# A software-pipelined graph-attention and expert kernel: other ranks for its phases, a lazier start, and a tail that begins one pair and one dense job per step

## The chip, the cores and the metric

The kernel runs on one NeuronCore of a Trainium2 chip. The metric is the time on the device in microseconds, from the first to the last instruction of the slowest (here the only) core; the time of a kernel is the median of several executions.

## The reference

Two layers are applied to x, 64 batches of 256 nodes with 256 features. `adj` is one 256 x 256 adjacency matrix for all batches. Cut to what matters:

```python
x = x + L0_gnn(layernorm(x), adj, W0, a0)     # 4 heads of 64, leaky slope 0.2, ELU at the end
x = x + layernorm(x) @ weight.T + bias        # 256 -> 256
x = x + L1_gnn(layernorm(x), adj, W1, a1)     # 1 head of 256, slope 0.01, ReLU at the end
x = x + L1_ffn(layernorm(x), router, w1, b1, w2, b2)

def gnn(h, adj, W, a):                        # per head
    q = h @ W
    e = leaky_relu(q @ a_src [:, None] + q @ a_dst [None, :])
    attn = softmax(where(adj, e, -huge), axis=-1)
    return act(attn @ q)

def L1_ffn(tokens, router, w1, b1, w2, b2):   # 8 experts, the best two of each token
    probs = softmax(tokens @ router.T); rw, re = top_k(probs, 2); rw = rw / rw.sum(-1)
    out = tokens
    for e in range(8):
        out = out + combine[:, e] * (gelu(tokens @ w1[e] + b1[e]) @ w2[e] + b2[e])
```

All is in float32.

## The kernel before

**Two kinds of work.** 62 of the 64 batches are *routed*: after the layers their rows are sent by indirect transfers to a buffer in device memory, `xs`, ordered by expert. Each token appears there twice. From that buffer *pairs* of tiles (256 rows of one expert) are read, run through the expert and added into the output rows by indirect transfers that add. There are 131 pairs. The last two batches are *dense*: every one of the 8 experts is applied to all of their rows, and the products are summed on chip, which makes 16 dense jobs.

**Steps, jobs and ranks.** Nothing is left to a scheduler. Each batch, pair or dense job is a Python generator; a loop of steps advances every active generator by one piece per step. What a generator yields is its *rank* in the next step: pieces of one step are emitted in the order of their ranks, smaller ones first, and jobs of equal rank in the order in which they began. The order of emission is the order on each engine's queue. A batch begins in every third step (`TICKS = 3`, in the step with phase 2), so in one step seven or so batches are worked on, each three pieces behind the one before it.

The pieces of a batch (`batch_layers`) and the step phase in which each falls, with the names that the profile shows:

| piece | phase | what it does | main instructions |
|---|---|---|---|
| 0 | 2 | transpose of the loaded blocks | DVE xT<-xblk L447 |
| 1 | 0 | statistics of x0 | DVE L314, L315; POOL rstd L322, L323 |
| 2 | 1 | projection of layer 0, then exp and scaling | PE pq L343; ACT q L351; DVE q L355 |
| 3, 4 | 2, 0 | scores of heads 0 and 1, of heads 2 and 3 | PE pd L410; DVE z L417 |
| 5 | 1 | attention times values, division | PE pv L431; DVE rinv L438, hp L464 |
| 6 | 2 | ELU and residual: x1, and x1 with the bias | ACT e L470; DVE x L473, L474, x1b L476 |
| 7 | 0 | statistics of x1, its transpose | PE pt L329; ACT xT L333 |
| 8 | 1 | the linear layer: x2, its statistics | PE pf L484; DVE x L490 |
| 9 | 2 | transpose of x2 | PE pt L329; ACT xT L333 |
| 10 | 0 | projection of layer 1 | PE pq L375; ACT ex L382, q L383, me L388 |
| 11, 12 | 1, 2 | scores and attention of layer 1 | PE pd L394, pv L431; DVE z L399 |
| 13, 14 | 0, 1 | ReLU; residual and statistics | ACT rel L506; DVE x L510 |
| 15, 16 | 2, 0 | scale and shift; normalized rows xng, and base | DVE by L515; ACT L524, L529 |
| 17, 18 | 1, 2 | base to the output, transpose of xng; logits | PE pt L329, pl L550; DVE lg L554 |

After piece 18 the last batch of a chunk routes the chunk (`route`): the two best experts of each token (`top_two`, some 12 small VectorE instructions), positions and pair numbers (some 50 more), then two sends per 128 rows on GpSimd (L816). Most chunks have four batches.

A pair (`expert_pair`) takes a load of its rows xr (L674), one step later a load of the expert's weights we (L685), then the transposes px (L692) and ScalarE's copy sT (L696), `hidden` (PE ph L724, ACT hT L730), `result` (PE py L739, DVE y L745), the scaling of y (ACT L717), and two adding scatters (POOL L756). Both scatters of a pair wait until the two scatters before them have landed, since rows may repeat from pair to pair. There are 7 buffers for y, 5 for xr and 7 for weights. A dense job (`dense_expert`) loads weights, runs `hidden` and `result`, and adds into `base` (DVE L782).

**The loop.** In a step of phase 2 it begins a batch, up to two waiting pairs (three once all batches have begun) and up to two dense jobs.

PSUM is one ring of 8 banks, taken in turn by pq, pd, pv, pt, pf, pl, ph, py and px.

**Before the loop** the masks, both layers' weights with their score columns (`gnn_weights`), the linear weights' transpose (`wfT`) and the router's transpose are prepared, all ahead of the first batch.

Of the kernel before, what the change touches and what calls it, by code (L numbers as in the profile page):

```python
# [20 lines left out]
def rows_to_all(ap: bass.AP, n: int) -> bass.AP:  # L21

    return bass.AP(tensor=ap.tensor, offset=ap.offset, ap=[[0, P], [1, n]])
# [3 lines left out]
def kernel(  # L27
# [84 lines left out]
    AHEAD, BLOCKS_AHEAD = 3, 2  # L112
    xblk = {0: load_blocks(0)}
    xin = {0: load_batch(0)}

# [12 lines left out]

    masks = []
    for layer, op in enumerate((ALU.is_gt, ALU.not_equal)):  # L130
        mf = work.tile([P, NT, N], F32, tag="xT", name=f"maskf{layer}", bufs=4)
        nc.vector.tensor_scalar(mf, adj_i, 0.0, None, op0=op)
        pm = bank("pm", [NT, N])
        for t in range(NT):
            for j in range(NT):
                nc.tensor.transpose(
                    pm[:, j, t * P : (t + 1) * P], mf[:, t, j * P : (j + 1) * P], ident
                )
        m = const.tile([P, NT, N], F32, tag=f"mask{layer}", name=f"mask{layer}")
        nc.vector.tensor_copy(m, pm)  # L140
        masks.append(m)

# [9 lines left out]
    def gnn_weights(w, a, heads, slope, name):  # L152

        d = D // heads
        wx = const.tile([P, KT, heads, d + 3], F32, tag=name, name=name)  # L160
        for k in range(KT):
            nc.sync.dma_start(
                out=wx[:, k, :, :d],
                in_=w[k * P : (k + 1) * P, :].rearrange("p (h d) -> p h d", h=heads),
            )
        av = work.tile([P, 2, d], F32, tag="e", name=name + "_a", bufs=1)
        nc.scalar.dma_start(out=av.rearrange("p s d -> p (s d)"), in_=rows_to_all(a, 2 * d))
        prod = work.tile([P, heads, d], F32, tag="hp", name=name + "_p", bufs=1)
        for k in range(KT):
            for s, c in ((0, d + 1), (1, d)):  # L170
                nc.vector.tensor_mul(
                    prod, wx[:, k, :, :d], av[:, s : s + 1, :].to_broadcast([P, heads, d])
                )
                nc.vector.tensor_reduce(wx[:, k, :, c : c + 1], prod, AX.X, ALU.add)
            nc.vector.tensor_scalar(
                wx[:, k, :, d + 1 : d + 2], wx[:, k, :, d + 1 : d + 2], 1.0 - slope, None,
                op0=ALU.mult,
            )
            nc.vector.tensor_scalar(
                wx[:, k, :, d + 2 : d + 3], wx[:, k, :, d : d + 1], slope - 1.0, None,  # L180
                op0=ALU.mult,
            )
        flat = wx.rearrange("p k h c -> p k (h c)")
        center(flat, heads * (d + 3))
        return flat

    wx0 = gnn_weights(w0, a0, H, SLOPE0, "wx0")
    wx1 = gnn_weights(w1g, a1g, 1, SLOPE1, "wx1")

# [4 lines left out]
    wfT = const.tile([P, KT, D], F32, tag="wfT", name="wfT")  # L194
    pw = bank("pw", [KT, D])
    for t in range(KT):
        for k in range(KT):
            nc.tensor.transpose(
                pw[:, k, t * P : (t + 1) * P], wf_in[:, t, k * P : (k + 1) * P], ident
            )  # L200
    nc.vector.tensor_copy(wfT, pw)
    center(wfT, D)

    bias_f = const.tile([P, D], F32, tag="bias_f", name="bias_f")
    nc.scalar.dma_start(out=bias_f, in_=rows_to_all(bf, D))
    nc.vector.tensor_scalar(bias_f, bias_f, -1.0, None, op0=ALU.add)

    r_in = work.tile([E, D], F32, tag="x1b", name="r_in", bufs=1)
    nc.scalar.dma_start(out=r_in, in_=router)
    rT = const.tile([P, KT, E], F32, tag="rT", name="rT")  # L210
    pr = bank("pr", [KT, E])
    for k in range(KT):
        nc.tensor.transpose(pr[:, k, :], r_in[:, k * P : (k + 1) * P], ident[:E, :E])
    nc.vector.tensor_copy(rT, pr)

# [41 lines left out]
    def fill_spare():  # L257
# [8 lines left out]
        yield 90  # L266


    setup = [lambda e=e: pack_expert(e) for e in range(E)] + [fill_spare]

# [65 lines left out]
    def projected(xT, wx, heads, rstd):  # L336
# [13 lines left out]
        for t, pq in enumerate(pqs):  # L350
            nc.scalar.activation(  # L351
                q[:, t, :, d:], pq[:, :, d:], AF.Exp, scale=rstd[:, t : t + 1]
            )
        for t, pq in enumerate(pqs):
            nc.vector.scalar_tensor_tensor(  # L355
                q[:, t, :, :d], pq[:, :, :d], rstd[:, t : t + 1],
                q[:, t, :, d : d + 1].to_broadcast([P, heads, d]), op0=ALU.mult, op1=ALU.mult,
            )
        return q

# [80 lines left out]
    def batch_layers(b, c0, xng, lg):  # L441
# [5 lines left out]
        nc.vector.transpose(xT.rearrange("p k n -> p (k n)"), xb.rearrange("p k n -> p (k n)"))  # L447
        yield 15
        x0 = xin.pop(b)
# [3 lines left out]
        yield 20  # L453
        q = projected(xT, wx0, H, rstd)
        yield 10
# [7 lines left out]
        for t, pv in enumerate(pvs):  # L463
# [3 lines left out]
            )  # L467
        yield 20
        ex = work.tile([P, NT, D], F32, tag="e", name="e", bufs=1)
# [26 lines left out]
        xT = transposed(x2)  # L496
        yield 40
        q, ex, me = projected1(xT, rstd, b)
        yield 10
        z = scores1(ex, me)  # L500
# [32 lines left out]
        xng.append(xe)  # L533
        yield 35
        if not dense:
# [9 lines left out]
        xT = transposed(xe[:, :, :D], *(("xTd", DENSE) if dense else ()))  # L545
        yield 50
        pl = bank("pl", [NT, E])
# [111 lines left out]
    def expert_pair(j, n, ids, ef, regs, needs):  # L659
# [27 lines left out]
        )  # L687
        yield 40
        px = bank("px", [KT, PAIR])
# [114 lines left out]
    active = []  # L804
    waiting, dense_jobs = [], []
    sent = []

    def begin(job, rank):
        active.append([rank, len(order), job])
        order.append(job)  # L810
# [16 lines left out]
    def later(rank):  # L827

        yield rank
        while (len(order_steps) - 1) % TICKS == 0:  # L830
            yield rank

    def route(c, row0, nt, n, last, xng, lg):

        rt = lambda shape, name, bufs=2, dt=F32: chunk_tile(shape, name, c, bufs, dt)
        vec, tt = nc.vector, nc.vector.tensor_tensor
        ohs, first, ed = top_two(c, nt, lg)
        m = rt([E, nt], "m")
# [131 lines left out]
    batches = jobs()  # L970
    step, more, credit = 0, True, 0.0
    SETUP_AT = 4
    with tc.manual_schedule():
        while more or active or waiting or dense_jobs or scatters:
            phase = step % TICKS
            if phase == 2 and more:
                nxt = next(batches, None)
                more = nxt is not None
                if more:
                    begin(nxt, 25)  # L980
            if step >= SETUP_AT and setup:
                begin(setup.pop(0)(), 90)
            if phase == 2:
                credit = min(credit + (2.0 if more else 3.0), 3.0)
# [12 lines left out]
            order_steps.append(step)  # L997
            for entry in sorted(active, key=lambda a: a[:2]):
                entry[0] = next(entry[2], None)
            if half_done:  # L1000
                finish_norms(NT)
            active[:] = [a for a in active if a[0] is not None]
            step += 1

# [34 lines left out]
```

The softmax here doesn't subtract the row's maximum and nothing guards it: scores larger than these inputs give would overflow.

## Time and profile before

| | |
|---|---|
| median of 3 executions | 1779.86 us (1778.52 to 1787.77) |
| span of the profiled execution | 1763.1 us, mean granted TensorE clock 0.945 |
| PE (TensorE) busy | 1559.9 us, 88% |
| PEld (weight loads, overlapping PE) | 1379.3 us, 78% |
| DVE (VectorE) busy | 1286.8 us, 73% |
| ACT (ScalarE) busy | 898.6 us, 51% |
| POOL (GpSimd) busy | 840.5 us, 48% |
| the first projection on TensorE (L343) starts | 27.25 us |
| the last send (L816) starts | 1537.86 us |

In the profile's lines PE is TensorE, PEld its weight loads, DVE VectorE, ACT ScalarE, POOL GpSimd and SP SyncE, which issues most loads. "L474" is a line of the kernel. A timeline row has its start, the busy time, engine, line, operation, output<-inputs and a count; in brackets stands the idle time just before it and who ended it. A row of waits reads: who waited for whom, microseconds in total, times, longest. Busy time of TensorE is no measure of peak speed, since matmuls overlap.

### The profile page before, as it was taken

The page shows a single profiled execution, that of the slowest core. Times are in us where ns is not written, and L with a number is a line of the kernel's source. Part 1 is how long each engine was busy: PE and PEld are TensorE (multiplying, and loading weights), DVE is VectorE, ACT ScalarE, POOL GpSimd, SP SyncE. Part 2 cuts the span into 40 slices and gives each one's busy share as a digit, 9 for nine tenths or more (in the row PEclk, how much of TensorE's full clock was granted, in tenths as well). Part 3 has the DMA queues.
Part 4 walks back from the last instruction along what each step waited for, and adds up shares of the span by engine and source line. Part 5 has one row for each costly group of instructions (what it writes and reads, how often), then busy time and mean ns, then how long its engine had stood idle before and what let it go on. Part 6 is the DMA issues. An engine that isn't in the chain of part 4 may idle for free. (4 is left out here: it accounts for less than half of the span.)

```text
span 1763.1 us, 29661 instructions
## 1 busy us (share of the span) xinstructions
PE 1559.9 (88%) x8998; PEld 1379.3 (78%) x8998; DVE 1286.8 (73%) x4744; ACT 898.6 (51%) x1965; POOL 840.5 (48%) x790
## 2 busy tenths in 40 slices
PE   5788788789999999999999999999989999678792
PEld 4677677678898979898888888888878888567682
DVE  4788888888878787879796878789888876522231
ACT  0234333445565656565656565656556566443241
POOL 0111233434646565646464555646565555734444
PEclk8899888999999999999999999999999899888896
DMA  5611122344656555555555564645564446585663
GB/s 139 183 37 47 50 67 77 76 119 97 137 124 139 130 138 125 119 136 112 130 123 139 123 148 112 150 113 126 128 147 119 101 111 152 126 219 116 146 132 44
DMA packets 272542, 209.67 MB, mean 119 GB/s; under 512 B 153849, under 2 KB 226561, under 8 KB 272385
## 3 DMA queue, kind: packets, MB, share of 16 engines
q1 hardware_dynamic: 221760, 139.40, 28.9%
q0 software_dynamic: 49632, 67.39, 20.7%
q8 instruction: 74, 1.21, 0.3%
q10 hardware_dynamic: 992, 0.99, 0.2%
q14 instruction: 84, 0.68, 0.1%
HBM read 118.55 MB, written 89.15 MB: 118 GB/s over the span
## 5 line engine op out<-in xcount | busy, mean ns | idle before, releaser
L756 POOL DMA_INDIRECT out_dram<-y,to x262 | 420.2, 1604 | 323.5 <-DMA out_dram<-y,to 124.8
L431 PE MATMUL pv<-q,z 128*128 128x65 f32 (+1 forms) x2560 | 371.4, 301 | 9.2 <-DVE y L745 9.1
L431 PEld LDWEIGHTS pv<-q,z 128*128 128x128 f32 x2560 | 341.3, 197 | 26.1 <-DVE y L745 11.1
L322 POOL TENSOR_SCALAR rstd<-mv 128x4 f32<-128x4 f32 (+1 forms) x132 | 46.3, 350 | 511.8 <-DVE mv L315 420.2
L724 PE MATMUL ph<-sT,we 128*128 128x256 f32 x1048 | 251.0, 396 | 41.3 <-ACT sT L696 22.8
L816 POOL DMA_INDIRECT xs<-xng,pos x248 | 251.0, 1012 | 69.1 <-issue 67.5
L739 PE MATMUL py<-w2s,hT 128*128 (+1 forms) x1176 | 264.3, 380 | 0.0
L724 PEld LDWEIGHTS ph<-sT,we 128*128 128x128 f32 x1048 | 204.8, 200 | 71.0 <-ACT sT L696 23.7
L739 PEld LDWEIGHTS py<-w2s,hT 128*128 128x128 f32 x1176 | 223.9, 191 | 30.7
L417 DVE SCALAR_TENSOR_TENSOR z<-pd,q,mask 128x256 f32<-128x256 f32 x512 | 209.8, 472 | 6.8 <-PE pd L410 6.8
L745 DVE TENSOR_TENSOR y<-py,b2s 128x512 f32<-128x512 f32 x147 | 98.2, 689 | 150.3 <-PE py L739 96.3
L730 ACT ACTIVATE hT<-ph,we 128x256 f32<-128x256 f32 x294 | 123.2, 470 | 165.6 <-PE ph L724 125.8
L333 ACT COPY xT<-pt 128x512 f32<-128x512 f32 x192 | 112.1, 584 | 162.7 <-PE pt L329 162.7
L717 ACT ACTIVATE y<-y,w 128x256 f32<-128x256 f32 x262 | 113.4, 500 | 119.4 <-DVE y L745 119.4
L314 DVE BATCH_NORM_STATS2 stats<-x 128x6 f32<-128x256 f32 x384 | 155.0, 404 | 2.2
L329 PE MATMUL pt<-ident,x 128*128 128x128 f32 x512 | 85.9, 292 | 75.7 <-DVE x L474 73.9
L375 PE MATMUL pq<-wx,xT 128*128 128x259 f32 x512 | 140.4, 422 | 0.9 <-ACT xT L333 0.9
L323 POOL TENSOR_TENSOR rstd<-rstd,mhalf 128x4 f32<-128x4 f32 (+1 forms) x132 | 135.4, 1025 | 11.0
L343 PE MATMUL pq<-wx,xT 128*128 128x268 f32 x512 | 130.0, 398 | 2.3 <-DVE wt L226 2.3
L484 PE MATMUL pf<-wfT,xT 128*128 128x256 f32 x512 | 131.7, 403 | 0.0
L329 PEld LDWEIGHTS pt<-ident,x 128*128 128x128 f32 x512 | 62.7, 156 | 85.8 <-issue 42.1
L470 ACT ACTIVATE e<-hp 128x512 f32<-128x512 f32 x64 | 40.3, 630 | 160.4 <-DVE hp L464 160.4
(155 smaller groups left out, 2488.5 us busy)
## 6 DMA issues: line engine op xcount, KB each, us to landing
we<-wpack SPq DMA_DIRECT2D x147, 288.0 KB, 5.2
xr<-xs SPq DMA_DIRECT2D x131, 260.0 KB, 3.7
xblk<-in_x_dram SPq DMA_DIRECT2D x256, 64.0 KB, 3.6
xin<-in_x_dram SPq DMA_DIRECT2D x64, 256.0 KB, 4.1
out_dram<-base SPq DMA_DIRECT2D x64, 256.0 KB, 3.6
out_dram<-y,to POOLq DMA_INDIRECT x262, 4.3
xs<-xng,pos POOLq DMA_INDIRECT x248, 2.6
xs<-fill SPq DMA_DIRECT2D x9, 260.0 KB, 4.3
```

The source lines that it names most:

```text
L314: nc.vector.bn_stats(stats[:, t, :], src[:, t, :])
L323: nc.gpsimd.tensor_tensor(rstd[:, :n], rstd[:, :n], mhalf[:, :n], ALU.pow)
L329: nc.tensor.transpose(pt[:, k, t * P : (t + 1) * P], src[:, t, k * P : (k + 1) * P], ident)
L343: nc.tensor.matmul(pq.rearrange("p h c -> p (h c)"), xT[:, k, t * P : (t + 1) * P], wx[:, k, :], start=(k == 0), stop=(k == KT - 1),)
L375: nc.tensor.matmul(pq, xT[:, k, t * P : (t + 1) * P], wx1[:, k, :], start=(k == 0), stop=(k == KT - 1),)
L417: nc.vector.scalar_tensor_tensor(z[:, j, :], pd[:, i, :], q[:, j, h, d + 2 : d + 3], mask[:, j, :], op0=ALU.max, op1=ALU.mult,)
L431: nc.tensor.matmul(pv[:, h, :], z[:, j, t * P : (t + 1) * P], q[:, j, h, : d + 1], start=(j == 0), stop=(j == NT - 1),)
L484: nc.tensor.matmul(pf[:, t, :], xT[:, k, t * P : (t + 1) * P], wfT[:, k, :], start=(k == 0), stop=(k == KT - 1),)
L724: nc.tensor.matmul(ph[:, f, :], we[:, k * D + f * P : k * D + (f + 1) * P], xT[:, k, :], start=(k == 0), stop=(k == KT - 1),)
L739: nc.tensor.matmul(py[:, t, :], hT[:, f, t * P : (t + 1) * P], w2s[:, e, f * D : (f + 1) * D].rearrange("p e c -> p (e c)"), start=(f == 0 ...
L756: d = nc.gpsimd.indirect_dma_start(out=out_rows, out_offset=bass.IndirectOffsetOnAxis(ap=to[:, t : t + 1], axis=0), in_=y[:, t, :], in_off ...
L816: d = nc.gpsimd.indirect_dma_start(out=xs_d[: E * CAP * PAIR, :], out_offset=bass.IndirectOffsetOnAxis(ap=at, axis=0), in_=xe, in_offset=None,
```

## The change

Three things are edited.

1. *Other ranks.* Several pieces get another rank, so that the order within a step changes. The pieces, their contents and their step phases stay. In phase 2 the ELU and residual (piece 6) now come first, ahead of the scores; the logits come ahead of layer 1's attention; `top_two` goes to the end of the step. In phase 0 layer 1's projection comes ahead of the transpose of x1, and the statistics of x1 ahead of those of x0. In phase 1 layer 0's projection comes ahead of layer 1's scores, the scaling of q behind them (a negative rank: the job is put back into the same step's queue), attention comes ahead of the transposes of xng and of the pairs' rows.
2. *A lazier start.* The layer-0 weights are loaded before the first blocks of x; the linear weights, layer 1's score columns, the second mask and the router are prepared as jobs of the first steps, beside the first batch, and the packing of the experts begins three jobs later.
3. *The tail.* Once every batch has left its layers, each step begins one waiting pair and one dense job, where before up to three pairs and two dense jobs began in every third step.

```diff
@@ batch_layers
         nc.vector.transpose(xT.rearrange("p k n -> p (k n)"), xb.rearrange("p k n -> p (k n)"))
-        yield 15
+        yield 40
...
-        q = projected(xT, wx0, H, rstd)
+        q, pqs = projected(xT, wx0, H, rstd)
+        yield -28
+        scaled(q, pqs, H, rstd)
         yield 10
...
-        yield 20
+        yield 5
         ex = work.tile([P, NT, D], F32, tag="e", name="e", bufs=1)
...
         xT = transposed(x2)
-        yield 40
+        yield 20
         q, ex, me = projected1(xT, rstd, b)
-        yield 10
+        yield 25
         z = scores1(ex, me)
...
         xng.append(xe)
-        yield 35
+        yield 55
...
         xT = transposed(xe[:, :, :D], *(("xTd", DENSE) if dense else ()))
-        yield 50
+        yield 35
@@ expert_pair
-        yield 40
+        yield 60
         px = bank("px", [KT, PAIR])
@@ route
+        yield -90
         ohs, first, ed = top_two(c, nt, lg)
@@ before the loop
-    setup = [lambda e=e: pack_expert(e) for e in range(E)] + [fill_spare]
+    setup = [
+        lambda work=work: once(work)
+        for work in (prepare_f, prepare1, lambda: fill_mask(1, ALU.not_equal), prepare_r)
+    ]
+    setup += [lambda e=e: pack_expert(e) for e in range(E)] + [fill_spare]
...
-    wx0 = gnn_weights(w0, a0, H, SLOPE0, "wx0")
-    wx1 = gnn_weights(w1g, a1g, 1, SLOPE1, "wx1")
+    wx0, prepare0 = gnn_weights(w0, a0, H, SLOPE0, "wx0")
+    xblk = {0: load_blocks(0)}
+    xin = {0: load_batch(0)}
+    prepare0()
+    wx1, prepare1 = gnn_weights(w1g, a1g, 1, SLOPE1, "wx1")
@@ the loop
-    step, more, credit = 0, True, 0.0
-    SETUP_AT = 4
+    step, more, credit = 2, True, 0.0
+    SETUP_AT = 3
...
-            if phase == 2:
+            if not more and not layers:
+
+                for jobs_left in (waiting, dense_jobs):
+                    if jobs_left:
+                        begin(jobs_left.pop(0)(), 90)
+            elif phase == 2:
                 credit = min(credit + (2.0 if more else 3.0), 3.0)
...
-            for entry in sorted(active, key=lambda a: a[:2]):
+            queue = [(a[0], a[1], a) for a in active]
+            heapq.heapify(queue)
+            while queue:
+                *_, entry = heapq.heappop(queue)
                 entry[0] = next(entry[2], None)
+                if entry[0] is not None and entry[0] < 0:
+                    entry[0] = -entry[0]
+                    heapq.heappush(queue, (entry[0], entry[1], entry))
```

## The prediction

> **What bounds the kernel now.** I read the page's slices first (where is an engine full), then the busy time by stretch, TensorE's own waits, the timeline of one batch before the experts begin, and the chain of waits at the end.
>
> The page's slices:
> ```profile
> PE   5788788789999999999999999999989999678792
> ...
> DVE  4788888888878787879796878789888876522231
> ```
> TensorE (PE) is the fullest engine from the tenth slice on. Before that it is at 7 or 8 tenths, with VectorE (DVE) as full as it.
>
> Busy time by stretch; I cut at the batches' hp multiplies (L464), at the last send and at the last matmul:
> ```profile
> 43.30:106.80 63.50, 51.29 (x295) 43.91 (x294) 48.63 (x145) 18.05 (x46) 8.20 (x14) 0.88 0.52 136
> 106.80:177.70 70.90, 59.76 (x388) 52.34 (x387) 59.37 (x191) 28.99 (x73) 10.06 (x16) 1.00 0.21 48
> 177.70:381.60 203.90, 166.26 (x976) 143.52 (x976) 170.31 (x622) 79.83 (x192) 65.63 (x78) 0.88 0.28 75
> 381.60:1440.00 1058.40, 1015.37 (x6103) 910.15 (x6102) 869.46 (x3206) 638.15 (x1367) 592.32 (x544) 0.98 0.53 126
> ...
> 1541.00:1727.00 186.00, 157.17 (x730) 136.48 (x730) 52.89 (x168) 71.38 (x159) 79.56 (x51) 0.90 0.65 148
> ```
> The columns are length, PE, PE weight load, DVE, ACT, POOL, clock, DMA. TensorE idles 12.2 + 11.1 + 37.6 = 61 us in the first three, 43 us in the long fourth (4%: TensorE is the bound there), and 29 us in the tail.
>
> TensorE's waits:
> ```profile
> PE pt L329 <- DVE x L474: 73.9, 37, 5.7
> ...
> PE px L692 <- DMA xr<-xs: 11.3, 15, 1.7
> PE pv L431 <- DVE y L745: 9.1, 11, 1.8
> PE pd L394 <- ACT ex L382: 9.0, 37, 0.4
> ```
> One wait stands out: the transpose of x1 waits for VectorE to finish x1. The timeline of one batch shows why:
> ```profile
> 128.39 1.62 DVE L417 SCALAR_TENSOR_TENSOR z<-pd,q,mask 128x256 f32<-128x256 f32 x4
> ...
> 130.95 0.69 DVE L474 SCALAR_TENSOR_TENSOR x<-e,x 128x512 f32<-128x512 f32 x1
> ...
> 131.79 0.63 PE L329 MATMUL pt<-ident,x 128*128 128x128 f32 x4 [2.15 <-DVE x L474]
> ...
> 141.25 0.18 DVE L438 RECIPROCAL rinv<-pv 128x4 f32<-128x4 f32 x1 [1.58 <-PE pv L431]
> ```
> VectorE does four score products (1.62 us) before x1, TensorE stands 2.15 us, and later VectorE stands 1.06 us for q's exponential (L355, further down the same timeline) and 1.58 us for TensorE's pv. Neither is full: the loop pv, hp, x1, transpose, pv (7.7 us on VectorE, 9.5 on TensorE) sets the 17.25 us of a batch.
>
> The end of the chain of waits:
> ```profile
> 1739.47 0.71 issue
> 1740.19 1.55 POOL out_dram L756
> 1741.74 0.30 issue
> 1742.04 3.85 DMA out_dram<-y,to
> ```
> Each pair's two adding scatters wait for those before them: 1.55 + 0.30 + 3.8 + 0.8 = 6.45 us a pair.
>
> **What the Trainium skill says.** "TensorE: Matmul & The Clock Gate", step-by-step of a matmul: only weight loads are pulled ahead, matmuls stay in program order. The trace agrees: pq (L375) stood behind the waiting transpose though its xT was copied at 129.82. So the order of emission matters. Same page, clock gate: after an idle window of about 3.4 us the clock halves. The trace agrees in sign: clock 1.00 where the gaps are 2.15 us, 0.88 at 177.7 to 381.6, where gaps of 5.71 and 3.52 us occur. "PSUM — Partial Sum Buffer", specifications: 8 banks, all of which the kernel rotates through, so a matmul also waits for the reader eight allocations back. "DMA: Bandwidth & Descriptors", anatomy of a SWDGE DMA: a fixed part of some 2 us, mostly the write receipt, which fits a scatter chain that more work elsewhere cannot shorten; here a landing takes 3.8 us.
>
> **The change, part by part.** The order of instructions in the two built programs shows what moves. No arithmetic of a batch, pair or dense job is added or removed.
>
> *x1 moves ahead of the score products (rank 20 to 5), and the second projection pq ahead of x1's transpose (40 to 20 against 30).* x1 is ready 1.62 + 0.3 us earlier, and needed 1.9 us later (pq is 8 matmuls, 1.92 us in the timeline). 3.8 us covers the usual gaps of 0.64 to 2.2 us and most of the 5.7. The whole row of 73.9 us should nearly go.
>
> *What takes its place.* pq now follows the transpose of x2 with only four pd transposes (0.44 us) between, and needs ScalarE's copy of it: about 0.67 us where the two stood next to each other (at 1470), so 0.23 to 0.35 us a batch; the low end is 15 us over 64 batches, the high end 22. I take 0.3: 19 us, 13 of it in the stretch 381.6 to 1440. The scores' product now waits in VectorE's order behind x1, but its reader pv comes two steps later: nothing.
>
> *pv ahead of the transposes of xng and px (35 to 55, 40 to 60).* pv's banks now follow those of the projection, not those of py, so its wait for y (9.1 us) goes. px runs some 4 us later relative to its load, so the 11.3 us on xr mostly go. pd (L394) runs after the other projection, and its 9.0 us go. q's scaling (the negative rank) still stands behind the scores product, with the same 1.06 us for ScalarE. In this step the projected and attended batches differ, so pv does not wait for it.
>
> *Stretch 43 to 382.* Batches without routing: VectorE's floor is 17.25 - 3.09 idle + 1.06 = 15.2 us, TensorE's 14.5 + 0.3; together about 15.7, 1.5 less a batch, 10 us for seven. With routing, four batches take 79.7 us now with VectorE busy 66.2; its floor with 1.06 each is 70.4, and I take 74: 5.6 per four, 14 us for ten batches. Sum 24; nothing extra for the clock.
>
> *Stretch 382 to 1440.* Four batches take 92.4 us, TensorE busy 88.5. Of 3.9 idle I expect 1.7 to stay (0.3 each, and VectorE full in the routing batch): 2.2 times 11 is 24 us; I take 22.
>
> *Start.* The first projection ran at 27.25. Now the layer-0 weights are loaded first, and the wf, wx1, mask1 and router preparations run as jobs beside batch 0. The projection can start near 15, but VectorE must still do wx1 (about 4.4 us in the old timeline) and mask1 before the second score products; pv starts near 32 instead of 36.3. 4 us.
>
> *Tail.* 31 pairs go through the scatter chain after 1539; 30 steps of 6.45 are 193.5 us, they took 214. So 20 us are gaps, mostly where a burst of three filled the y buffers and the queue of loads stood behind (TensorE 11.6 us at 1655, 8.0 at 1603). One pair and one dense job a step spreads this: SyncE's load waits no longer hold five weight loads. But a step then costs TensorE 3.94 + 3.50 = 7.44 us for one pair while the 14 remaining dense jobs last, 1 us more than the chain, hidden only by queued pairs. Ends: 20 gained, 0 or a few lost. I take 8.
>
> Sum: 24 + 22 + 4 + 8 = 58 us of 1780: 1722.
>
> **Rivals.** (a) *The wait moves.* TensorE's new wait for the copy costs 0.67 instead of 0.3 (24 us more), or VectorE, with 170 of 204 us busy, is the true bound early, and gains there halve (12): 58 - 36 leaves 22, about 1758. For it: VectorE idles only 1.83 us in the routing batches; against: in three of four it has 2.7 to 7.7 spare. (b) *More than the sum.* All of TensorE's waits go and the clock stays up: 61 + 43 less 10 for the floor, less 19 for the copies, plus 10 for throttling and 10 in the tail: 95 us, 1685. For it: the clock of 0.88; against: VectorE's floor. (c) *Slower.* The tail becomes TensorE's (14 us) and its gaps stay, the copy wait is paid in every batch (0.67 x 64 = 43), x1's gap is only half gained (37): 1780 + 14 + 43 - 37 = 1800. For it: the chain has no slack in the end; against: x1 moves by 3.8 us.
>
> **How the numbers follow.** Forecast 0.52, (a) 0.28, (b) 0.10, (c) or no change 0.10. Range: from 1690, near (b), to 1768, above (a) with a tail that gains nothing; it leaves out (c) and part of (b), about 0.2. Faster by over 0.5% means under 1771: 0.87; within 0.05; slower 0.08.
>
> **What would show it.** Right: TensorE's wait for x1 falls from 74 us to under 15; a new row, pq behind ScalarE's xT, of 10 to 25 us; the stretch of 44 full batches shrinks by about 22 us and a batch before routing to about 15.7; the first pv near 32; scatter starts in the tail 6.4 to 7.5 us apart for each pair. Wrong: a wait of pv or pq above 1 us in every batch, VectorE with no idle time in the full stretch, or a tail over 222 us from the last send to the end.

## The result and the profile after

The changed kernel takes **1724.09 us** (median of 4, 1719.65 to 1725.74) beside 1781.0 for the kernel before (4 executions in all): a ratio of **0.967, 95% interval 0.964 to 0.970**. The forecast of 1722 holds, but not all of its terms do.

The page's slices of the changed kernel, TensorE, VectorE and the granted clock:
```profile
PE   5999889899999999999999999999999998699870
...
DVE  6889898978787878878787878788788966423220
...
PEclk8999989899999999999999999999999999899995
```
TensorE is now at 8 or 9 tenths from the second slice on, and was so before only from the tenth. The weak place is left at the end.

Busy time by stretch, cut at the same events (start, hp of the batches 4, 8, 18 and 63, last send, end); columns as before:
```profile
0.00:38.50 38.50, 22.10 (x85) 16.41 (x86) 21.57 (x70) 2.15 (x5) 3.99 (x20) 0.82 0.48 108
38.50:96.40 57.90, 48.40 (x292) 41.60 (x291) 48.30 (x148) 17.25 (x45) 10.65 (x14) 0.94 0.66 179
96.40:161.90 65.50, 61.77 (x382) 53.70 (x381) 58.72 (x190) 29.85 (x74) 13.12 (x16) 0.97 0.23 52
161.90:349.20 187.30, 166.28 (x974) 143.06 (x973) 167.40 (x613) 77.63 (x189) 70.15 (x78) 0.93 0.28 73
349.20:1390.30 1041.10, 1005.08 (x6093) 897.14 (x6093) 860.96 (x3203) 636.97 (x1367) 613.20 (x543) 0.99 0.56 130
...
1488.00:1724.00 236.00, 163.19 (x771) 138.65 (x769) 58.50 (x191) 70.90 (x163) 97.47 (x63) 0.87 0.58 125
```
Against before, the start gives 43.3 - 38.5 = 4.8 us, the next three stretches 338.3 - 310.7 = 27.6, the full stretch 1057.8 - 1041.1 = 16.7; the tail from the last send to the end **grew** from 225.2 to 236.0, by 10.8. Together that is 39 us, and the medians differ by 57: the profiled execution of the kernel before, 1764.81 us, lies 16 us under the median (first experiment).

TensorE's waits:
```profile
...
PE pt L351 <- DVE by L545: 21.6, 20, 4.2
PE pq L400 <- ACT xT L355: 14.0, 55, 0.7
...
PE px L719 <- DMA xr<-xs: 8.0, 10, 1.5
...
PE pv L456 <- DVE z L442: 5.6, 5, 2.2
...
PE pt L351 <- DVE x L501: 1.7, 1, 1.7
```
The row of 73.9 us for x1 (now L501) is down to 1.7 in one wait. The new row for ScalarE's copy is there, 0.25 us each. The rows for pv on y and pd on ex are gone. The first row shown was not forecast. It is the transpose of x1 again, and `by`, which the profile names, is nothing that it reads. Each of the twenty waits ends 2.44 us after x1 and 0.15 us after the scores' product (L442), as before the change it ended 0.15 us after x1 (131.64 to 131.79). Counted in the ring of eight PSUM banks, the transpose at 135.71 takes the bank of the pd at 128.70, which this product frees at 135.56. So a part of the wait most likely moved from x1 to the product that was put behind x1; no run tests this.

Two steps of the tail in which a pair and a dense job begin together, in the chain of waits:
```profile
1598.44 0.15 issue
1598.59 6.32 DMA out_dram<-y,to
...
1607.39 0.16 issue
1607.55 6.16 DMA out_dram<-y,to
```
A second scatter lands after 6.2 to 6.3 us here, where the prediction's chain had 3.85. With the 2.63 us from a landing to the next pair's second scatter that makes 8.9 us a pair. Eight steps in a row take 8.0 to 10.4 us so (1580 to 1651 us); the last seven, with no load beside them, take 6.3 to 6.5 again.

### The profile page after: what moved, and what is told of

It reads as the page before. It is cut to its first block, busy times and chain, and to the rows that moved or that the text cites. A ratio compares the mean times of both kernels' runs of the same rounds, so it can differ in the third digit from the quotient of the medians.

```text
span 1724.0 us, 29724 instructions
## 1 busy us (share of the span) xinstructions
PE 1548.5 (90%) x8998; PEld 1362.0 (79%) x8998; DVE 1276.3 (74%) x4744; ACT 895.0 (52%) x1965; POOL 872.0 (51%) x790
## 5 line engine op out<-in xcount | busy, mean ns | idle before, releaser
L456 PE MATMUL pv<-q,z 128*128 128x65 f32 (+1 forms) x2560 | 376.2, 302 | 8.5 <-DVE z L442 5.6
L456 PEld LDWEIGHTS pv<-q,z 128*128 128x128 f32 x2560 | 336.7, 196 | 22.4 <-DVE z L442 6.3
L344 POOL TENSOR_SCALAR rstd<-mv 128x4 f32<-128x4 f32 (+1 forms) x132 | 63.2, 478 | 436.8 <-DVE mv L337 356.4
L751 PEld LDWEIGHTS ph<-sT,we 128*128 128x128 f32 x1048 | 200.1, 196 | 69.2 <-ACT sT L723 33.3
L766 PEld LDWEIGHTS py<-w2s,hT 128*128 128x128 f32 x1176 | 218.1, 190 | 27.2 <-issue 0.3
L442 DVE SCALAR_TENSOR_TENSOR z<-pd,q,mask 128x256 f32<-128x256 f32 x512 | 210.9, 473 | 6.6 <-PE pd L435 6.5
L345 POOL TENSOR_TENSOR rstd<-rstd,mhalf 128x4 f32<-128x4 f32 (+1 forms) x132 | 157.1, 1190 | 11.0
L400 PE MATMUL pq<-wx,xT 128*128 128x259 f32 x512 | 129.2, 394 | 16.1 <-ACT xT L355 14.0
L365 PE MATMUL pq<-wx,xT 128*128 128x268 f32 x512 | 135.7, 411 | 8.4 <-DVE wt L239 4.2
L400 PEld LDWEIGHTS pq<-wx,xT 128*128 128x128 f32 x512 | 91.9, 189 | 42.8 <-ACT xT L355 27.3
L365 PEld LDWEIGHTS pq<-wx,xT 128*128 128x128 f32 x512 | 100.9, 200 | 30.2 <-issue 7.6
L533 ACT ACTIVATE rel<-pv,rinv 128x256 f32<-128x256 f32 x128 | 53.9, 473 | 117.3 <-DVE rinv L463 100.7
```

The lines of the kernel that those rows point to most:

```text
L345: nc.gpsimd.tensor_tensor(rstd[:, :n], rstd[:, :n], mhalf[:, :n], ALU.pow)
L365: nc.tensor.matmul(pq.rearrange("p h c -> p (h c)"), xT[:, k, t * P : (t + 1) * P], wx[:, k, :], start=(k == 0), stop=(k == KT - 1),)
L400: nc.tensor.matmul(pq, xT[:, k, t * P : (t + 1) * P], wx1[:, k, :], start=(k == 0), stop=(k == KT - 1),)
L442: nc.vector.scalar_tensor_tensor(z[:, j, :], pd[:, i, :], q[:, j, h, d + 2 : d + 3], mask[:, j, :], op0=ALU.max, op1=ALU.mult,)
L456: nc.tensor.matmul(pv[:, h, :], z[:, j, t * P : (t + 1) * P], q[:, j, h, : d + 1], start=(j == 0), stop=(j == NT - 1),)
L751: nc.tensor.matmul(ph[:, f, :], we[:, k * D + f * P : k * D + (f + 1) * P], xT[:, k, :], start=(k == 0), stop=(k == KT - 1),)
```

## The experiments

Line numbers are those of each kernel. All but the first were timed in three rounds; each ratio is to the kernel before on the same chip and at the same time. The kernel before itself had medians of 1781, 1783, 1759, 1786 and 1782 us in the five comparisons, so times of different comparisons are not subtracted; stretches of the profiles are.

**1. Where the two numbers for before part.** The kernel before, not edited.

> The kernel before, profiled once more. The three parts of the two profiles (to batch 4's hp, layers, tail) differ by 39 us (-10, -49, +11 and rests), the medians by 57. Theory: the first profile of the kernel before (span 1763) was an execution with fewer throttled stretches, and another execution spends some 15 us more, in the stretch before the experts (43 to 382), at a granted clock below 0.945; the tail of 225 us from the last send stays. Rival: the tail also differs by 10 us or more from execution to execution, so that 225 against 236 us between the two kernels says nothing.

1806 us. The stretches, in order: 43.3, 63.6, 70.8, 204.2, 1098.2, 96.4, 227.8. Its full stretch:
```profile
381.93:1480.15 1098.22, 1048.70 (x6101) 937.45 (x6100) 868.21 (x3204) 637.35 (x1366) 590.38 (x542) 0.95 0.52 122
```
All but 1 us of the 41 by which this span exceeds the first sits here: 40.5 us longer, TensorE busy for 34 more with as many matmuls, at a clock of 0.95 for 0.98. The clock record shows why: within this stretch the clock stood at half for 34.1 us in the first profile and for 102.4 in the second, and half of the difference is the 34 us. The gaps were alike. TensorE's wait of 0.76 us for the experts' y comes nine times in each profile; half clock followed it three times in the first and eight times in the second. So I had the place wrong (not the early batches, which repeat to 0.3 us). The rival on the tail falls too: 2.5 us between the two executions against the 10.8 at issue. The kernel before pays a varying bill for half-clock time in its full stretch, and the part of the 57 us that the profiles leave out probably lies there. No median execution was profiled, but the seven executions timed beside this one agree: those of 1773 and 1775 us had a clock of 0.946 and 0.947, the two of 1796 us 0.936 and 0.937.

**2. The old rule for the tail.**
```diff
-            if not more and not layers:
-                for jobs_left in (waiting, dense_jobs):
-                    if jobs_left:
-                        begin(jobs_left.pop(0)(), 90)
-            elif phase == 2:
+            if phase == 2:
```


> The changed kernel with the old rule for the tail (up to three pairs and two dense jobs in every third step). Theory (the new tail loses time: a step's three loads slow its own scatters): some 10 us faster than the changed kernel, about 1714, the tail from the last send to the end 225 instead of 236 us. Prediction on record (the tail gains 8): about 1732. Rival (the longer tail comes from something else in the change, for example more pairs waiting when the sends end): 1724, the tail still 236.

1715.6 us, ratio 0.962 (0.955 to 0.970). The tail is 225.2 us. A piece of its chain, in which no load is issued:
```profile
1583.64 3.78 DMA out_dram<-y,to
...
1588.20 1.55 POOL out_dram L783
1589.75 0.30 issue
1590.06 3.84 DMA out_dram<-y,to
```
The landing is back to 3.8 us. In the nine profiles with the old rule, here and below, the tail takes 224 to 228 us, in the five with the new one 230 to 236.

**3. The ranks alone** (in the kernel before: all the new ranks, old start, old tail).

> The kernel before with the new ranks alone; old start, old tail. Theory: the ranks are the whole gain of the layers: 1781 - 46 = about 1735, the wait for x1 under 10 us, 15.6 us a batch before routing. If the start and the tail matter in sum (prediction: -12) it lies 12 above the changed kernel, 1736; if they cancel (-4 and +11, as the profiles say) it is equal to or a little under the changed kernel, 1717 to 1724.

1718.6 us, ratio 0.962 (0.954 to 0.970). The stretches are 43.9, 56.9, 65.5, 187.8, 1042.0, 98.7, 226.3: the layers as in the changed kernel. The ranks are the whole gain: beside this profile, that of the changed kernel has 5.5 us less at the start and 9.8 more in the tail, and its span is 3 us longer.

**4. x1 first: two ranks alone**, the two that the prediction priced at the whole row of 73.9 us.
```diff
@@ batch_layers, in the kernel before
-        yield 20
+        yield 5
         ex = work.tile([P, NT, D], F32, tag="e", name="e", bufs=1)
...
         xT = transposed(x2)
-        yield 40
+        yield 20
         q, ex, me = projected1(xT, rstd, b)
```


> The kernel before with two ranks alone: x1 ahead of the scores (20 to 5) and layer 1's projection ahead of x1's transpose (40 to 20). Theory (these two make nearly all of the gain of the ranks): the wait for x1 (73.9 us) gone, about 1745, batches before routing about 15.7 us. Rival (the gain needs the others too: projection and attention ahead, q's scaling late, or else the wait moves to pv behind q): gain halved, about 1765, and pv or pt waits over 1 us in each batch.

**1825 us, slower**: ratio 1.021 (1.012 to 1.030). The wait for x1 is gone (1.7 us), and it bought little where it had stood: the stretches from 43 to 382 take 332.3 us in place of 338.3. Two things show why. First, VectorE in a batch that does not route, before the experts begin:
```profile
152.23 0.88 DVE L355 SCALAR_TENSOR_TENSOR q<-pq,rstd,q 128x256 f32<-128x256 f32 x2 [1.06 <-ACT q L351]
153.02 0.17 DVE L438 RECIPROCAL rinv<-pv 128x4 f32<-128x4 f32 x1
154.77 0.18 DVE L438 RECIPROCAL rinv<-pv 128x4 f32<-128x4 f32 x1 [1.58 <-PE pv L431]
```
The same 1.06 + 1.58 us of idle time as before the change, and nearly the same time a batch (17.17 us for 17.26): the x1 wait was slack of TensorE in a loop whose pace VectorE set. TensorE now stands 1.12 us for ScalarE's ex instead, and pv comes no earlier.

Second, the full stretch, and three windows in it:
```profile
549.44:566.51 17.07, 14.62 (x80) 11.47 (x78) 12.94 (x39) 10.73 (x22) 13.88 (x12) 1.00 0.50 102
566.51:580.16 13.65, 12.65 (x50) 11.77 (x51) 5.99 (x24) 4.28 (x8) 3.19 (x2) 0.50 0.66 152
580.16:593.80 13.64, 13.40 (x72) 11.75 (x72) 9.18 (x29) 5.55 (x12) 10.04 (x10) 1.00 0.51 150
```
```profile
567.51 1.08 PE L692 MATMUL px<-ident,xr 128*128 128x128 f32 x4 [2.48 <-DMA xr<-xs]
568.39 6.93 PE L431 MATMUL pv<-q,z 128*128 128x65 f32 x32
575.11 3.72 PE L484 MATMUL pf<-wfT,xT 128*128 128x256 f32 x8
```
TensorE reaches px before its rows are there, idles 2.48 us, and the clock is halved for 13.65 us: the pv group takes 6.93 us where it takes 3.68 at full clock. This comes back in nearly every four batches, and each of the nine waits of 0.76 us is now followed by half clock: 150.2 us of it in the stretch, which lasts 1131 us with TensorE *busy* for 1078, against 1005 in the changed kernel. A gap alone does not do it: in the batches before routing of the kernel before, the gaps of 2.15 us left the clock at 1.00 (the row 106.80:177.70 of the prediction).

**5. Also the scores of layer 1 behind the projection.**
```diff
@@ batch_layers, in experiment 4
-        yield 10
+        yield 25
         z = scores1(ex, me)
```


> The kernel with x1 first (two ranks, 1825 us) plus one more: layer 1's scores behind layer 0's projection (rank 10 to 25). There the wait for x1 was gone and the batches before routing still took 17.6 us, with the transposes of ex waiting 0.7 us each, up to 2.5, for ScalarE. Theory (that wait had taken x1's place early): the row of 21.5 us falls under 5, the four batches to the ninth take 66 to 67 us instead of 70.5, the ten with routing some 190 instead of 199; the full stretch stays near 1130; about 1808 in all. Rival (VectorE's own order, with q's scaling ahead of attention, sets the pace early): 70.5 stays and the row moves to another.

1847.9 us, ratio 1.030 (1.022 to 1.039): no gain, as the rival said, and even longer (72.1 us for the four batches, 212.4 for the ten). TensorE's wait for ex went, one for xng took its place (19.1 us), and VectorE only redistributes its idle time:
```profile
152.16 0.88 DVE L355 SCALAR_TENSOR_TENSOR q<-pq,rstd,q 128x256 f32<-128x256 f32 x2 [1.83 <-ACT q L351]
...
154.71 0.18 DVE L438 RECIPROCAL rinv<-pv 128x4 f32<-128x4 f32 x1 [0.80 <-PE pv L431]
```
1.83 + 0.80 us is again 2.63. The scores' product had stood between the projection and q's scaling; behind it, q's scaling waits the longer for ScalarE.

**6. Attention ahead of the transposes instead.**
```diff
@@ batch_layers and expert_pair, in experiment 4
-        yield 35
+        yield 55
...
-        yield 50
+        yield 35
...
-        yield 40
+        yield 60
         px = bank("px", [KT, PAIR])
```


> The kernel with x1 first (1825 us) plus attention ahead of the transposes of xng and of the pairs' rows (35 to 55, 40 to 60, logits 50 to 35). In the full stretch it had two gaps in every four batches, 0.76 us (attention on the experts' y) and 2.5 us (px on the loaded rows), and the clock fell to half for 3 to 14 us right behind each: 1131 us at a mean clock of 0.93. Theory (gaps of 1 to 2.5 us are enough to halve the clock, and these ranks remove them): the stretch falls to about 1045 at a clock of 0.98 or more, about 1740 in all, with the batches before routing unchanged at 17.6 us. Rival (the clock falls for some other reason, as the density of the work): it stays below 0.95 and the stretch above 1090.

1753.6 us, ratio 0.981 (0.975 to 0.986). The full stretch, and VectorE early:
```profile
370.81:1425.02 1054.21, 1013.09 (x6099) 901.94 (x6098) 861.78 (x3203) 638.11 (x1367) 615.90 (x544) 0.99 0.54 128
```
```profile
148.70 0.88 DVE L355 SCALAR_TENSOR_TENSOR q<-pq,rstd,q 128x256 f32<-128x256 f32 x2 [1.06 <-ACT q L351]
149.49 0.17 DVE L438 RECIPROCAL rinv<-pv 128x4 f32<-128x4 f32 x1
150.40 0.18 DVE L438 RECIPROCAL rinv<-pv 128x4 f32<-128x4 f32 x1 [0.73 <-PE pv L431]
```
The wait of px on its rows is down to 2.9 us in all, half clock from 150.2 us to 23.9, and 77 us of the 1131 are gone, with the same matmuls. The four early batches take 70.7 us (17.7 each), unchanged as expected, but only because two effects cancel. A batch that does not route went from 17.2 to 16.3 us, since pv comes 0.85 us earlier; the batch that routes gave this back, with 21.7 us for 19.0:
```profile
162.11 0.16 DVE L595 TENSOR_TENSOR ed<-top,top 128x8 f32<-128x8 f32 x1
...
162.37 0.23 DVE L438 RECIPROCAL rinv<-pv 128x1 f32<-128x1 f32 x2
...
163.60 0.99 PE L394 MATMUL pd<-ident,ex 128*128 128x128 f32 x2 [4.29 <-ACT ex L382]
```
With the logits' new rank `top_two` (L578 to L595) comes ahead of layer 1's reciprocal on VectorE. ScalarE's ReLU waits for the reciprocal, its ex stands behind the ReLU, and TensorE stands 4.29 us. In the changed kernel `top_two` is late, and the order is right again:
```profile
151.85 0.21 DVE L463 RECIPROCAL rinv<-pv 128x1 f32<-128x1 f32 x2
151.99 0.19 DVE L605 TENSOR_REDUCE top<-lg 128x8 f32<-128x64 f32 x1
```
There the batch takes 18.9 us.

**7. Six ranks**: 4, 5 and 6 together.

> The kernel before with six ranks: x1 first (two), attention ahead of the transposes (three), and layer 1's scores behind layer 0's projection (10 to 25), which alone with x1 first gave nothing (17.17 us a batch before routing, VectorE idle 1.83 + 0.80 in each). Theory: the early batches are a loop through VectorE, its period is 14.5 us of work and its idle time; idle was 2.64 before, 1.80 with x1 first and px later, where attention's sum (rinv on pv) still waits 0.74 behind the transposes of ex. With the scores moved this goes: 1.06 us idle are left, 15.6 us a batch, 65.5 and about 188 us for the two stretches, the row of 44.4 us (pd on ex) under 5, a full stretch of about 1045, 1718 to 1728 in all. Rival (the split of q's scaling, the late statistics or the late top_two are needed): 16.3 us a batch, 1740 or more.

1760.4 us, ratio 0.987 (0.981 to 0.993): the rival's figures, 16.3 us a batch and over 1740. Of the theory one part came, the end of the wait for pv.
```profile
134.06 0.88 DVE L355 SCALAR_TENSOR_TENSOR q<-pq,rstd,q 128x256 f32<-128x256 f32 x2 [1.83 <-ACT q L351]
134.85 0.87 DVE L399 SCALAR_TENSOR_TENSOR z<-pd,ex,me 128x256 f32<-128x256 f32 x2
135.64 0.24 DVE L438 RECIPROCAL rinv<-pv 128x4 f32<-128x4 f32 x2
```
The wait for pv is gone, but q's scaling waits 1.83 us. In the changed kernel the piece is split by the negative rank:
```profile
124.57 0.86 DVE L424 SCALAR_TENSOR_TENSOR z<-pd,ex,me 128x256 f32<-128x256 f32 x2
126.48 0.88 DVE L381 SCALAR_TENSOR_TENSOR q<-pq,rstd,q 128x256 f32<-128x256 f32 x2 [1.06 <-ACT q L373]
127.28 0.24 DVE L463 RECIPROCAL rinv<-pv 128x4 f32<-128x4 f32 x2
```
On TensorE the projection comes first and the scores' transposes second; on VectorE the scores' product comes first and q's scaling second. Only the split gives both orders. VectorE in a batch that does not route, before the experts begin:

| kernel | idle: q on exp + rinv on pv | period | period less idle |
|---|---|---|---|
| before | 1.06 + 1.58 | 17.26 | 14.62 |
| x1 first | 1.06 + 1.58 | 17.17 | 14.53 |
| and scores later | 1.83 + 0.80 | 17.16 | 14.53 |
| x1 first, attention ahead | 1.06 + 0.73 | 16.33 | 14.54 |
| six ranks | 1.83 + 0 | 16.32 | 14.49 |
| changed kernel | 1.06 + 0 | 15.56 | 14.50 |

(The period is from one scaling of q to the next.) Six kernels, one sum: 14.5 to 14.6 us of work and the idle time. Work and idle time add up to the period on any engine; what the table says is that VectorE has no third wait, and that the period moves only when one of these two does.

Over all batches of the stretches from 43 to 382 us the sums are 338.3 (before), 332.3 (x1 first), 330.8 (attention ahead as well), 330.0 (six ranks) and 310.7 (changed kernel). With six ranks, too, the batches that route have the order of experiment 6 (TensorE stands 2.11 us for ex, half clock follows, and the batch takes 20.9 us). So some 19 of the 27.6 us came only with the last three ranks: the split, the later `top_two` and the later statistics of x0. The full stretch is 1061 us with six ranks and 1042 with all. How these differences divide between the three was not tried; the lines above speak for the split in the batches that do not route and for `top_two` in those that do.

**8. The changed kernel again**, beside the next three.

> The changed kernel again, beside the next three on the same chip: 1720 to 1726 expected, a tail of 236 us from the last send. If it comes out near 1715, the 10 us between it and the old tail rule were between two chips or moments and not of the rule.

1715.4 us, ratio 0.976 (0.973 to 0.979), the tail 234.3 us: the tail repeats, the level does not (full stretch 1025.5 instead of 1041.1 us). By what was written beforehand, the 10 us between the medians of this kernel and of experiment 2 are then not shown to be of the tail rule; what stays shown is the length of the tails, 224 to 228 against 230 to 236 us.

**9. Dense jobs without loads.**
```diff
-        we = io.tile([P, WROW], F32, tag="we", name="we", bufs=WBUFS)
-        nc.sync.dma_start(out=we, in_=wpack[e])
...
-        hT = hidden(own["xT"], we)
+        hT = hidden(own["xT"], w2s[:, e, :], b2s[:, e, :2])
```


> The changed kernel in which the dense jobs load no weights and multiply with the second layer's weights that are resident in their place: 16 loads of 288 KB are left out, and the dense products are other ones, with the same number of matmuls. Theory T1 (a step's loads go out just behind its scatter and slow its landing): the second landing back from 6.2 to some 4 us, the steps with a dense job 7.4 to 7.6 instead of 8.0 to 10.4, the tail some 12 us shorter, about 1712. Rival T2 (TensorE with 7.44 us of work a step is the pace, or the ring of 7 y buffers that pairs and dense jobs share): steps stay near 8.9, landings may shorten, the time stays within 4 us of the changed kernel's.

1713.4 us, ratio 0.974 (0.971 to 0.977), the tail 230.1 us: 4 of the 12 us that I expected. The chain of waits there:
```profile
1598.40 5.11 DMA out_dram<-y,to
...
1606.15 5.98 DMA out_dram<-y,to
```
The pair's own two loads still go out within 1 us of each second scatter (at 1606.36 and 1606.96 for the one at 1606.15), so these two landings take 5.1 and 6.0 us. To separate the dose from the kernel I took, in the tails of nine profiles (the kernel before and the changed one twice each, experiments 2, 3, 9, 10 and 11), the time from a second scatter to the next pair's first, where a landing ended the wait, by the number of loads issued from 1 us before to 2.5 us after it:

| loads beside it | 0 | 1 | 2 | 3 | 4 | 5 | 6 |
|---|---|---|---|---|---|---|---|
| mean, us | 4.61 | 4.93 | 6.02 | 6.89 | 7.14 | 8.39 | 7.35 |
| cases | 108 | 19 | 22 | 19 | 15 | 8 | 7 |

So loads beside a scatter go with a slower landing, also where all of them are the pair's own. Two or three in one step after another cost 1.4 to 2.3 us each time; five or six in a burst 2.7 to 3.8 once, and the scatters between bursts run at 4.6. The time itself stayed within 4 us of the changed kernel's, as the rival said. Its reason is out: TensorE's 7.44 us are under the 7.7 to 9.5 that the eight slow steps in a row take here (1573 to 1640 us). Each of these steps ends on a landing, and the next scatter starts 0.8 us after it, as where no load is near, so that its y was ready.

**10. A dense job in every second step.**
```diff
-                for jobs_left in (waiting, dense_jobs):
+                alternate = [dense_jobs] if step % 2 == 0 or not waiting else []
+                for jobs_left in [waiting, *alternate]:
```


> The changed kernel, with a dense job begun only in every second step of the tail as long as pairs wait. By T1 and by the pace of TensorE alike a pair's step should cost 6.5 to 7.5 us instead of 8.9: two steps have 2 x 3.94 + 3.50 = 11.4 us of TensorE and five loads in place of six. Expected: the tail 12 to 20 us shorter than 236, about 1708. If the scatters' own chain of 6.45 us is never the pace, or the last dense jobs come to stand after the last pair: no gain or a loss.

1717.6 us, ratio 0.978 (0.975 to 0.980): no gain, the tail 233.7 us. Steps of 6.4 us now stand among the others, but loads pile up in some of them (four beside one scatter in four cases, 7.5 us), and others take up to 10.3. Fewer loads in a step are not enough; which scatter they meet is not set by this.

**11. x2's transpose earlier**, against the new wait for ScalarE's copy.
```diff
         _, rstd = norm_stats(x2)
-        yield 60
+        yield 38
         xT = transposed(x2)
```


> The changed kernel with x2's transpose ahead of layer 0's attention (rank 60 to 38), so that ScalarE's copy has longer. The row of 14.0 us (layer 1's projection on ScalarE's xT, 55 times) should fall under 2. Theory (TensorE is the bound in the full stretch and each of its waits counts): 10 to 14 us less, about 1712. Rival (the 0.24 us are absorbed elsewhere, or x2's transpose now waits for VectorE's x2 and its statistics): no gain, and a new row for the transpose on x2 of 10 us or more.

**1705.2 us, 10 us under the changed kernel beside it** (ratios 0.971, 0.968 to 0.974, and 0.976, 0.973 to 0.979). Its waits:
```profile
...
PE pt L351 <- DVE by L545: 14.8, 22, 2.9
PE pt L351 <- DVE x L517: 10.2, 19, 1.9
PE pv L456 <- DVE z L442: 8.0, 7, 2.5
```
The row of 16.1 us that the changed kernel had beside it is gone; the rival's row on x2 (L517) has come as well, with 10.2. The two profiles lie 12.4 us apart. Of these, 6.8 are in the full stretch (1018.7 against 1025.5); 4.1 are in the second stretch (57.1 against 61.2), where the changed kernel had 57.9 in its first profile, so that they are not shown to be of this edit.

**12. Both repairs.** Experiments 2 and 11 together.

> The changed kernel with the two repairs together: the old rule for the tail (-9 by the profiles) and x2's transpose ahead of layer 0's attention (-10 measured). Theory (they lie in different stretches and add): 19 us under the changed kernel, 1696 to 1705 by chip, the tail 225 us. If the tail's length depends on how many pairs wait when the layers end: less than 15.

1711.3 us beside 1786 for the kernel before: ratio **0.956 (0.949 to 0.962)**, the lowest of all, and below the changed kernel's in both of its comparisons. Full stretch and tail:
```profile
347.18:1385.14 1037.96, 1005.99 (x6093) 900.07 (x6093) 863.56 (x3203) 641.73 (x1367) 614.03 (x544) 0.99 0.56 131
1485.68:1710.01 224.33, 164.13 (x772) 142.43 (x770) 59.39 (x191) 73.48 (x163) 97.72 (x63) 0.87 0.60 131
```
The tail is the old one. The full stretch is only 2.5 us under that of experiment 2, so the 19 us are not shown: 10 to 12 from the tail are, the rest is open, since the changed kernel did not run beside it.

## Why the prediction was right, and where not

*The total* was right by more than its terms deserve: 58 predicted, 57 measured, with a tail of the wrong sign, and a gain of half-clock time that was priced at nothing. In the two profiles from which the terms can be read the gain is 39; the rest is mostly that the first profile of the kernel before was a quick execution. That the sums agree so closely is luck.

*43 to 382: 24 predicted, 27.6 measured.* The floor was the right tool: VectorE's work plus the 1.06 us for ScalarE gave 15.2, the forecast 15.7 a batch, the trace 15.56. (The 15.2 took away also 0.45 us of short gaps between instructions, which stay.) But the step before it, "the whole row of 73.9 us should nearly go" as the source of the gain, named the wrong cause, and the loop through x1's transpose did not set the 17.25 us. In experiment 4 the row went, and with it 6.0 of 338 us. Attention ahead of the transposes and the scores later, which were listed as side effects, brought 2.3 us more by themselves. Some 19 came with the split of q's scaling, the later `top_two` and the later statistics, of which only the split stands in the prediction; that q would still wait only 1.06 us was predicted, and experiment 7 shows what it costs without the split.

*382 to 1440: 22 predicted, 16.7 in the two profiles*, and 57 against the second profile of before. The forecast took idle time off, 22 us. TensorE's idle time fell by 7.0 only (43.0 to 36.0), since new waits came, and its busy time by 9.6 (1014.7 to 1005.1), which no term had. Here the missing term is the clock. In the kernel before and in experiment 4 an idle gap of 0.8 to 2.5 us was often followed by 3 to 14 us at half clock, and removing the gap removed both: half clock takes 34.1 and 102.4 us of this stretch in the two profiles of before, 11.0 and 3.4 in those of the changed kernel. The Trainium skill, "TensorE: Matmul & The Clock Gate", part on the clock gate, says that the clock drops after an idle window of about 3.4 us. The trace disagrees on the gap needed: in experiment 4 a gap of 2.48 us, and one of 0.76 us that ended at 544.41, were followed by half clock (for the second from 546.03 to 549.44). Its granularity agrees: up to the end of the layers the half-clock stretches of the clock record last 3.41 us or a multiple of it. Over the whole span the granted clock went from 0.945 to 0.959, that is 97 to 71 us of full-clock time withheld (span x (1 - clock)). "Nothing extra for the clock" in the early stretches is open: half clock takes 63.2 us of them before and 37.5 after, but VectorE sets the pace there, and what this gave was not separated.

*The copy: 0.3 us a batch predicted, 0.25 measured* (14.0 us in 55 waits), a row of 14 in the range of 10 to 25. Experiment 11 removes the row and is 10 us shorter. The scores' product behind x1 was priced at nothing; the new row of 21.6 us for x1's transpose most likely comes from it.

*The rows of pv on y and of pd on ex* went as said. px on xr fell from 11.3 to 8.0, and to 2.8 in the second profile.

*Start: 4 predicted, 4.8 measured.* The first projection at 15.71 (near 15), the first pv at 34.66 (32 was forecast).

*Tail: 8 gained predicted, 10.8 lost.* The failed step is "Ends: 20 gained, 0 or a few lost". The 20 us of gaps were there, but were put down to full y buffers and a queue of loads, and the 6.45 us chain was taken as fixed, "a scatter chain that more work elsewhere cannot shorten"; whether traffic can lengthen it was not asked. It does, and did so before the change, for example behind the second scatter of 1550.14, with five loads beside it:
```profile
1558.64 1.55 POOL L756 DMA_INDIRECT out_dram<-y,to  x1 [6.95 <-DMA out_dram<-y,to]
```
Without loads this wait is about 3.0 us. Spreading the work put loads beside eight scatters in a row, and their landings went from 3.85 to some 5.4 to 7.8 us. A tail over 222 us was named as a sign of error, and it is one; so are the scatter starts, 6.3 to 10.5 us apart for each pair in place of 6.4 to 7.5.

*Rivals.* Of (a), VectorE is indeed the bound early, as the table of idle times shows, but the gain there was not halved: the batches came down to its work and the 1.06 us. (b) saw that the clock matters. (c) saw that the tail could lose, for the wrong reason: TensorE's 7.44 us never became the pace.

## What to carry to other kernels

A long row of waits on the fullest engine is a price only if that engine sets the pace of its loop: take the wait away alone and see whether the period moves, or add up for the other engine its work and its idle time, as here 14.5 + 2.6 us, and ask what ends each idle piece. Where order is written by hand, two engines may want opposite orders of the same two pieces; splitting a piece so that each engine's half has its own place took 0.77 us of waiting from a batch. A rank that helps most batches can hurt the one that does more, as the early logits did where a batch routes. A chain of dependent transfers has a length that depends on what is in flight beside it, so spreading loads evenly can cost more than bursts.

## What was not expected of the hardware

- A single TensorE gap of 0.76 us was followed by 3.4 us at half clock, one of 2.48 us by 13.65 us (experiment 4); whether a gap has this effect varied from one execution to the next (three and eight times in nine), and one kernel's full stretch took 1057.8 or 1098.2 us for it.
- In all fourteen traces the changes of the clock fall on one grid of 3.413 us that runs through the whole trace and does not start anew at a gap. Of the grid's intervals at full clock, counted up to the last matmul, half clock followed 167 of the 209 in which TensorE was busy for less than 40%, 126 of 1558 between 40 and 95%, and none of 4615 above. So an interval need not be empty. That the place of a gap on the grid decides what it does would fit the variation, but is not shown.
- The landing of a 128-row adding scatter took 3.8 us with nothing beside it and 5.1 to 6.3 us beside two or three loads of 260 to 288 KB, in the chains shown; on average one load cost 0.3 us, the second about 1.1.
- The same kernel came out at 1724 and 1715 us in two comparisons (the kernel before at 1781 and 1759), and its full stretch in the two profiles took 1041.1 and 1025.5 us, with half clock for 11.0 and 3.4 us of it.
